# Pairing the short last tiles of two experts in one turn of a mixture-of-experts kernel

## The chip, the cores and the metric

The kernel runs on one core of a Trainium2 chip. The core has five engines that work side by side, each through its own queue in its own order: TensorE (PE in the profile; its weight loads have a row of their own, PEld), VectorE (DVE), ScalarE (ACT), GpSimd (POOL) and SyncE (SP). They hand work to each other through semaphores; 16 DMA engines move data between the device memory and the on-chip memory, on queues that SP, ACT and POOL feed. The metric is device time in microseconds (us), the median of several executions. One further execution is recorded by the hardware profiler, and all rows below come from that one.

## The reference

The input x has 2 sequences of 2048 tokens, 256 features each, in fp32: 4096 tokens. Three blocks follow each other, each on a layer-normed x and added back to x:

```python
x = x + 0.5 * ffn(layernorm(x))
x = x + attn(layernorm(x))
x = x + 0.5 * ffn(layernorm(x))
```

`ffn` is a mixture of 8 experts with top-1 routing. A token's expert is the argmax of 8 router logits; its own layer norm, a 256 to 1024 matrix W1 with bias and relu, a 1024 to 256 matrix W2 with bias, and the router's probability as a gate follow, all of that one expert:

```python
idx = argmax(softmax(xt @ Wr + br));  gates = max(softmax(...))
h = relu(xn @ W1[idx] + b1[idx])
y = (h @ W2[idx] + b2[idx]) * gates
```

`attn` is no attention but three layers of a gated linear recurrence over time (short convolution, two gates from 64x64 matrices, a scan, an output matrix, an RMS norm), between a 256 to 64 and a 64 to 256 projection. It needs the tokens in their order of time, while the ffn needs them sorted by expert.

How many tokens an expert gets is known only at run time. On the inputs drawn here the router sends 332, 17, 1583, 15, 1969, 2, 0 and 178 tokens to the eight experts in the first ffn, and 265, 27, 1637, 9, 1972, 1, 0 and 185 in the second.

## The kernel before

**Turns.** An expert's tokens are cut into tiles of P = 128. A tile is worked off in one turn of the generator `expert_tiles` (L1124), in three steps. `gathered` (`fetched`, L764, then `turned`, L820) gathers the tile's rows and its expert's weights W1 (with both biases, 1.18 MB) by indirect DMAs from POOL, normalises the rows on ACT (`z`, L825), transposes them on TensorE (`tpe`, L828) and scales them on DVE into `xT`. `hidden` (L845) multiplies them by W1 into PSUM (`ph`, L854) and applies bias and relu, by turns on ACT (L866) and DVE (L868), into `hT`. `finish` (L871) multiplies by W2, which for all eight experts stays in SBUF as `w2_sb` and is addressed through a register (`py`, L879), adds the bias (L887), gates and adds the residual (L888), and scatters the rows to their tokens by an indirect DMA (L890). TensorE works in the order hidden(j+1), transposes of j+2, finish(j). Buffers: four W1 tiles (`wp`), four row tiles (`xes`, XB), two of each `hT`, `xT` and `z`, three PSUM banks for `ph`, one for `py`.

**How many turns.** `NJ` = 39 bounds the number of tiles that 4096 tokens of 8 experts can need. The first ffn always runs `SURE` = 37 turns, the second 37; two tiles that the first may have over share the first two turns of the second, and two more turns of the second stand in branches that run only if the count calls for them. So 74 turns run.

**Which rows.** `First` (L390) works out for the whole input, before any turn, which tokens fill which tile: logits, one-hot experts, counts and ranks by matrix products (`Ranks`, L300), a number for each tile in the order in which tiles are opened (`count`), and from it the tables `idx` (token of each row), `sidx` (row of its statistics in `x_stat`) and `wrow` (rows of W1). `Route` (L569) does the same for the second ffn, one group of 512 tokens at a time; `ready` turns as many tiles into tables as are sure to be full.

**The order of the work.** The recurrence goes through 8 groups (`Chunk`), of 256 steps of both sequences each. Group g loads its tokens from `x1`, the DRAM buffer that the first ffn's turns scatter to, after as many turns as are sure to hold all of its tokens (`opened_by`: 11, 15, 19, ...), then `LAG` = 2 more turns are written down, then the group's projection (`down`, L1010, with `pd`, L1024) and its three layers. The framework takes this program order as priority and fixes each engine's order when the kernel is built. What is left of the turns is written down after the last group. So the run has a front (routing, no turns), a stretch of turns alone, a middle in which turns fill TensorE between the recurrence's steps, and a tail of turns alone. Waiting instructions hold up all that stands behind them on their engine; on POOL those are the gathers and scatters of other turns.

**Matmuls narrower than the array.** Two places write only some of the 128 output partitions: the router's logits in quarters of 32 (L229) and `pd` in halves of 64 (L1024).

Of the kernel before, what the change touches and what calls it, by code (L numbers as in the profile page):

```python
# [21 lines left out]
G = 4  # L22
# [28 lines left out]
def opened_by(n):  # L51

    return min(NJ, (n + E * (P - 1)) // P)
# [12 lines left out]
OWN = 3  # L66
EARLY = filled_by((NG - 1) * G * P)


SPARE = 2  # L70
SURE = NJ - SPARE
NS = NJ + SPARE


@with_exitstack
def macaron_kernel(
# [4 lines left out]
    w2: bass.AP,  # L81
# [88 lines left out]
    XB = 4  # L170
# [72 lines left out]
    class Choice:  # L243
# [48 lines left out]
        def sums(self):  # L292

            ex = self.tile([P, self.M, E], "ex")
            self.exp = nc.scalar.activation(ex, self.lo, AF.Exp)
            nc.vector.tensor_reduce(self.m[:, 1, :], ex, AX.X, ALU.add)
            nc.vector.reciprocal(self.m[:, 1, :], self.m[:, 1, :])
            return self.m[:, 1, :]

    class Ranks:  # L300
# [4 lines left out]
        def __init__(self, tile, M, oh, tiles, at, number, zero_one, all_ones, rk):  # L305
# [20 lines left out]
            place = cnt[:, 1]  # L326
            now = self.now = tiles[:, :, 1 : 1 + M]
            nc.vector.tensor_scalar(now, cnt[:, 0], SHIFT, None, ALU.arith_shift_right)
            opened = tile([P, M, E], "opened")
            nc.vector.tensor_tensor(opened.rearrange("p i e -> p e i"), now, tiles[:, :, 0:M], ALU.subtract)  # L330
            count = self.count = tile([P, M, E], "count")
# [10 lines left out]
            )  # L342

# [18 lines left out]
    def sort_into(got, lh, i0, n, tiles, first_one, last_one):  # L362


        hit, col, row = tiles
        nc.vector.tensor_tensor(
            hit,
            lh[:, 0, :, None].to_broadcast([P, n, NJ]),
            iota[:, None, 1 : 1 + NJ].to_broadcast([P, n, NJ]),
# [11 lines left out]
        for i in range(n):  # L381
            nc.tensor.matmul(
                got[:, 0 : 2 * NJ],
# [6 lines left out]
    class First:  # L390
# [5 lines left out]
        def __init__(self, pool):  # L396
            self.stores = []
            self.w2 = []
# [20 lines left out]
            xgs = [group_tile(), xpool.tile([P, G, D], F32, tag="u", name="u", bufs=1)]  # L419
            xgs += [Lane(0).tile([P, G, D], "x1"), group_tile(), Lane(1).tile([P, G, D], "x1")]  # L420
            for k in (2, 1):
                both = wp.tile([P, W1ROW], F32, tag="w1", name="x67")
                xgs += [
                    both[:, i * G * D : (i + 1) * G * D].rearrange("p (n d) -> p n d", d=D) for i in range(k)
                ]
# [26 lines left out]
            r = Ranks(tile, M, oh, tiles, at, number, flat(zero_one), all_ones, rk)  # L452


            pairs = tile([P, M, E], "pairs")
# [14 lines left out]
            by_turn = tile([P, H, NJ], "by_turn")  # L470
            turns = lane.bank([P, NJ], "turns")
            for a in range(H):
                nc.vector.tensor_scalar(
                    by_turn[:, a, :],
                    iota[:, 1 : 1 + NJ],
# [10 lines left out]
            wrow = kept([P, NJ], "wrow")  # L486
# [4 lines left out]
            got = bank("py", [P, 2 * NJ], "got")  # L491
            n = 2 * G
            for i in range(0, M, n):
                pieces = (
                    pool.tile([P, n, NJ], BF16, tag="f_hit", name="hit", bufs=2),
                    pool.tile([P, n, 2, NJ], BF16, tag="f_col", name="col", bufs=2),
# [5 lines left out]
            token = tile([P, NJ], "token")  # L502
            nc.vector.tensor_scalar(token, got[:, 0:NJ], float(P), float(FAR), ALU.mult, ALU.add)
            idx = kept([P, NJ], "idx")
            nc.vector.tensor_tensor(idx, token, got[:, NJ : 2 * NJ], ALU.add)
            at_p = tile([P, NJ], "at_p")
            nc.vector.tensor_scalar(at_p, got[:, NJ : 2 * NJ], float(NT), 2.0 * NT, ALU.mult, ALU.add)
            sidx = kept([P, NJ], "sidx")
            nc.vector.tensor_tensor(sidx, at_p, got[:, 0:NJ], ALU.add)
# [18 lines left out]
            with tc.issue_after(r.found.ins):  # L528
# [5 lines left out]
            self.idx = [(idx[:, j : j + 1], NG - 1) for j in range(NJ)]  # L534
            self.sidx = [sidx[:, j : j + 1] for j in range(NJ)]
            self.wrow = [wrow[:, j : j + 1] for j in range(NJ)]
            self.w2at = [(w2at, j, SURE) for j in range(SURE)]

            nc.vector.scalar_tensor_tensor(
                sidx[:, SURE:NJ], idx[:, SURE:NJ], -float(T), sidx[:, SURE:NJ], ALU.add, ALU.max  # L540
            )
            self.late_wrow, self.late_at = wrow[:, SURE:NJ], at[:, SURE:NJ]
# [3 lines left out]
    def second_weights(turns, kept, late=None):  # L546
# [4 lines left out]
        if late is not None:  # L551
            nc.vector.scalar_tensor_tensor(
                at[:, 0:SPARE], turns[:, 0:SPARE], float(W2ROW // P), late, ALU.mult, ALU.add
            )
# [14 lines left out]
    class Route:  # L569
# [5 lines left out]
        def __init__(self):  # L575
            self.stores = []
            self.idx, self.wrow, self.w2at, self.w2 = [], [], [], []
# [16 lines left out]
        def add(self, g, xg):  # L594
# [51 lines left out]
            if last:  # L646
                n += E
                nc.vector.tensor_tensor(filled[:, M, :], tiles[:, :, M], fills[:, :, M], ALU.subtract)
                nc.vector.tensor_copy(pairs[:, 1, M, :], new[:, :, M])
# [14 lines left out]
            )  # L664
            slots_of = pairs[:, 1, 0:M, :].rearrange("p i e -> p e i")
# [15 lines left out]
            by_turn = lane.tile([(1 + M) * E, 2, NS], "by_turn")  # L681
            for a, v in ((0, cst[0:n, C_EV : C_EV + 1]), (1, of_pair[0:n, 1:2])):
                nc.vector.tensor_scalar(
                    by_turn[0:n, a, :],
                    iota[0:n, 1 + SURE : 1 + SURE + NS],
# [5 lines left out]
            got = lane.bank([P, 2 * NJ + 2 * NS], "got")  # L691
# [13 lines left out]
            new_sum = cpool.tile([P, 2 * NJ + 2 * NS], F32, tag=f"sum{g % 2}", name="sum")  # L705
# [10 lines left out]
        def ready(self, upto, group):  # L716
# [3 lines left out]
            if n <= 0:  # L720
                return

            def kept(shape, name, dt=I32):
                return cpool.tile(shape, dt, tag=f"{name}1_{j0}", name=name)

            wrow = kept([P, n], "wrow")
# [4 lines left out]
                self.turns[0:1, 0, j0:upto], kept, first.late_at if j0 == 0 else None  # L731
            )
            if j0 == 0:
# [532 lines left out]
```

## Time and profile before

| | us |
|---|---|
| median of 3 runs | 772.67 (771.89 to 780.03) |
| the profiled execution's own time | 772.9 |
| its span, first to last instruction | 770.9 |
| busy: PE / PEld / DVE / ACT / POOL | 705.9 / 618.8 / 453.2 / 343.8 / 312.8 |
| mean granted TensorE clock | 0.966 |

A matmul of fp32 is two records in the profile: `ph` has 2368 records for 74 turns (32 each) and `py` 1184 (16 each). A record's duration holds its latency; how fast they follow each other is read from the timeline, where a row gives the start, the length and how many records it merges ("x32"). A busy time is the union of its records. "[0.30 <-issue]" at a row's end is idle time of the engine before it and what ended it.

### The profile page before, as it was taken

Reading aid. Unit: us, or ns where it says so; the run is one execution under the profiler, and the core shown is the slowest. Engines: PE = TensorE matmul, PEld = TensorE weight load, DVE = VectorE, ACT = ScalarE, POOL = GpSimd, SP = SyncE. Lnnn points to the kernel's source line nnn. Section 1 sums busy time; section 2 is a strip of 40 time slices with the busy share of each in tenths; the row PEclk is TensorE's granted clock in tenths of the full one; section 3 lists DMA queues with packets and bytes.
Section 4 is the critical chain, followed back from the end, with each engine's and each line's share of the span. In section 5 each row is a group of like instructions: output and inputs, shape, how many; then the busy total and the mean of one; then the engine's idle time right before and its main releaser. Section 6 shows DMA issues by size and latency. Waiting matters only on the chain. (4 is left out here: it accounts for less than half of the span.)

```text
span 770.9 us, 14129 instructions
## 1 busy us (share of the span) xinstructions
PE 705.9 (92%) x4785; PEld 618.8 (80%) x4785; DVE 453.2 (59%) x1674; ACT 343.8 (45%) x772; POOL 312.8 (41%) x319
## 2 busy tenths in 40 slices
PE   9639999979999989999998898898999899999995
PEld 6438999968778878878886796787878898999994
DVE  7653434345588677686885866767668433344341
ACT  4323323226566753757656576455552222223220
POOL 4444555524434334353365333133432433434432
PEclk9859999989999999999999999899999999999998
DMA  9986555544526334263344534343533556455430
GB/s 332 408 219 206 171 201 210 181 153 145 177 80 207 148 131 148 77 225 122 131 164 158 171 116 138 104 151 109 211 129 135 194 190 218 163 219 193 164 127 8
DMA packets 36808, 129.75 MB, mean 168 GB/s; under 512 B 7282, under 2 KB 21888, under 8 KB 26240
## 3 DMA queue, kind: packets, MB, share of 16 engines
q0 software_dynamic: 19584, 104.51, 39.3%
q1 hardware_dynamic: 16720, 23.93, 9.1%
q8 instruction: 42, 0.69, 0.4%
q10 hardware_dynamic: 432, 0.37, 0.2%
q14 instruction: 30, 0.25, 0.1%
HBM read 118.19 MB, written 16.38 MB: 175 GB/s over the span
## 5 line engine op out<-in xcount | busy, mean ns | idle before, releaser
L854 PE MATMUL ph<-xT,w 128*128 128x128 f32 x2368 | 303.2, 281 | 2.1 <-ACT hT L866 1.0
L854 PEld LDWEIGHTS ph<-xT,w 128*128 128x128 f32 x2368 | 290.4, 195 | 13.4 <-issue 5.6
L879 PE MATMUL py<-w_sb,hT 128*128 x1184 | 280.5, 382 | 1.1 <-DVE ye L887 0.6
L879 PEld LDWEIGHTS py<-w_sb,hT 128*128 128x128 f32 x1184 | 215.8, 190 | 29.8 <-issue 4.4
L794 POOL DMA_INDIRECT w<-w_rows_dram,wrow x76 | 78.7, 1035 | 329.0 <-issue 142.1
L866 ACT ACTIVATE hT<-ph,w 128x128 f32<-128x128 f32 x296 | 106.7, 366 | 136.3 <-PE ph L854 69.3
L868 DVE TENSOR_SCALAR hT<-ph,w 128x128 f32<-128x128 f32 x296 | 102.0, 347 | 110.2 <-ACT hT L866 99.1
L825 ACT ACTIVATE z<-xe 128x256 f32<-128x256 f32 x74 | 44.3, 599 | 172.4 <-DMA xe<-xa,idx 88.0
L887 DVE TENSOR_TENSOR ye<-py,w 128x256 f32<-128x256 f32 x74 | 31.1, 421 | 77.3 <-PE py L879 66.9
L832 DVE TENSOR_SCALAR xT<-tpe,par 128x128 f32<-128x128 f32 x148 | 57.2, 404 | 25.5 <-PE tpe L828 25.2
L774 POOL DMA_INDIRECT xe<-x_in_dram,idx x39 | 42.3, 1084 | 24.7 <-issue 8.3
L890 POOL DMA_INDIRECT x<-ye,idx x39 | 40.7, 1045 | 20.2 <-issue 6.5
L890 POOL DMA_INDIRECT out_dram<-ye,idx x37 | 37.9, 1024 | 24.6 <-DVE ye L888 15.1
L774 POOL DMA_INDIRECT xe<-x_stat,sidx x39 | 39.6, 1017 | 14.2 <-issue 11.3
L774 POOL DMA_INDIRECT xe<-xa,idx x39 | 40.6, 1040 | 11.9 <-issue 10.7
L828 PE MATMUL tpe<-cst,z 128*128 128x128 f32 x148 | 29.3, 279 | 9.7 <-ACT z L825 9.7
L888 DVE SCALAR_TENSOR_TENSOR ye<-ye,xe 128x256 f32<-128x256 f32 x74 | 35.6, 481 | 1.6
L1047 DVE SCALAR_TENSOR_TENSOR xc<-xb,par,xc 128x256 f32<-128x256 f32 x72 | 34.5, 480 | 0.5
L1054 ACT ACT_TABLE_LOAD x21 | 26.9, 1283 | 13.3 <-PE pm L1052 11.5
L215 ACT COPY uT<-tp 128x512 f32<-128x512 f32 x40 | 22.4, 586 | 21.4 <-PE tp L213 21.1
L1067 ACT ACT_TABLE_LOAD x22 | 28.2, 1283 | 0.4
L828 PEld LDWEIGHTS tpe<-cst,z 128*128 128x128 f32 x148 | 18.8, 144 | 10.9 <-ACT z L825 10.7
(211 smaller groups left out, 740.2 us busy)
## 6 DMA issues: line engine op xcount, KB each, us to landing
w_sb<-w_dram SPq DMA_DIRECT2D x8, 1024.0 KB, 16.0
xa<-xg SPq DMA_DIRECT2D x16, 259.0 KB, 5.0
x<-x SPq DMA_DIRECT2D x16, 256.0 KB, 3.1
x<-x_in_dram SPq DMA_DIRECT2D x10, 256.0 KB, 5.5
xa<-cst SPq DMA_DIRECT2D x2, 1036.0 KB, 17.7
w<-w_rows_dram,wrow POOLq DMA_INDIRECT x76, 6.1
xg<-x_in_dram SPq DMA_DIRECT2D x4, 256.0 KB, 4.8
xe<-x_in_dram,idx POOLq DMA_INDIRECT x39, 4.1
```

The costliest lines, as they stand in the source:

```text
L774: got = nc.gpsimd.indirect_dma_start(out=xe[:, a:b], out_offset=None, in_=src, in_offset=bass.IndirectOffsetOnAxis(ap=at, axis=0), bounds_ ...
L794: nc.gpsimd.indirect_dma_start(out=w1[:], out_offset=None, in_=w1_rows, in_offset=bass.IndirectOffsetOnAxis(ap=r.wrow[j], axis=0), bounds_ ...
L825: nc.scalar.activation(z, xe[:, 0:D], AF.Identity, scale=scale, bias=shift)
L828: nc.tensor.transpose(tp[:, c, :], z[:, c * P : (c + 1) * P], ident)
L832: nc.vector.tensor_scalar(xT[:, c, :], tp[:, c, :], par[:, P_G + c : P_G + c + 1], par[:, P_B + c : P_B + c + 1], ALU.mult, ALU.add,)
L854: nc.tensor.matmul(ph[:, q, :], lhsT=w1[:, c * F + f * P : c * F + (f + 1) * P], rhs=xT[:, c, :], start=(c == 0), stop=(c == C - 1),)
L866: nc.scalar.activation(hT[:, f, :], ph[:, q, :], AF.Relu, bias=b1)
L868: nc.vector.tensor_scalar(hT[:, f, :], ph[:, q, :], b1, 0.0, ALU.add, ALU.max)
L879: nc.tensor.matmul(py, lhsT=hT[:, f, :], rhs=w2_sb[:, bass.ds(r.w2[j] + f * D, D)], start=(f == 0), stop=(f == FC - 1),)
L888: nc.vector.scalar_tensor_tensor(ye, ye, gate, xe[:, 0:D], ALU.mult, ALU.add)
L890: made = nc.gpsimd.indirect_dma_start(out=dst, out_offset=bass.IndirectOffsetOnAxis(ap=at, axis=0), in_=ye, in_offset=None, bounds_check=T ...
L1047: nc.vector.scalar_tensor_tensor(xc, self.xb[:, k : k + GT], cw(k), xc, ALU.mult, ALU.add)
```

## The change

Tiles that are the last of their expert and hold fewer than 64 tokens are *short*. Up to six short tiles per ffn are taken out of the ordinary numbering and put by twos into three *mixed* turns. In a mixed turn, rows 0 to 63 belong to one expert and rows 64 to 127 to another. Each matmul writes 64 output partitions, half of TensorE's columns: in `hidden` one per half of the hidden units and per expert, so 64 products with 64 stationary and 64 moving columns in place of 16 of 128 by 128; in `finish` 16 of 64 rows by 256 in place of 8. The first expert's W2 comes from `w2_sb`, the second's by a third gather, `w2b`, into a buffer of `wp`; a mixed turn so gathers 1.18 + 1.18 + 1.05 MB, and gathers and scatters its rows in halves, with an indirect DMA each.

With the mixed turns, `NF` = 35 bounds the ordinary tiles. The first ffn runs 31 ordinary and 3 mixed turns, the second 31 and 3; the rest stands in branches. On the inputs above either ffn has 37 tiles, six of them short: 31 and 3 hold them all. Mixed turns are the 5th, 8th and 11th turn of the first ffn, as their tokens may belong to any group, and stand among the last ten of the second. Group g is loaded after 14, 18, 22, ... turns.

Other parts: a turn's rows are issued a turn ahead of its weights (`rows`, `weights`, `then_weights`); XB is 5; the bias of W2 and the residual are combined before `py` is there, by a DVE operation at the end of `hidden` (it is then the W1 buffer's last reader), and one DVE operation is left after `py`; `LAG` is 1; `OWN`, the group from which tables of the second ffn are made, is 2 in place of 3; the front's scratch tiles share buffers in another way.

```diff
-OWN = 3
-SPARE = 2
-SURE = NJ - SPARE
-NS = NJ + SPARE
+OWN = 2
+HALF = P // 2
+MIXED = 3
+U = 2 * MIXED
+NF = (T + max(E * (HALF - 1), (E - U) * (P - 1))) // P
+NC = NF + U
+SPARE = 4
+SURE = NF - SPARE
+NS = NF + SPARE
+NSC = NS + U
+LAST = 31
...
-    XB = 4
+    XB, YB = 5, 5
...
+    def short_tiles(tile, held, now, start):
+        used = tile([P, E], "used")
+        nc.vector.scalar_tensor_tensor(used, now, -float(P), held, ALU.mult, ALU.add)
+        is_short = tile([P, E], "is_short")
+        nc.vector.tensor_scalar(is_short, used, float(HALF), None, ALU.is_lt)
+        nth = tile([P, E], "nth_short")
+        nc.vector.tensor_tensor_scan(nth, ones[:, 0:E], is_short, 0.0, ALU.mult, ALU.add)
+        paired, number = tile([P, E], "paired"), tile([P, E], "pair_at")
+        nc.vector.scalar_tensor_tensor(paired, nth, U + 0.5, is_short, ALU.is_lt, ALU.mult)
+        nc.vector.scalar_tensor_tensor(number, nth, float(start), paired, ALU.add, ALU.mult)
+        return paired, number
...
+            if short_from is not None:
+                paired, pair_at = short_tiles(tile, self.held, now[:, :, M - 1], short_from)
+                newest = tile([P, E], "newest")
+                nc.vector.tensor_tensor(newest, paired, now[:, :, M - 1], ALU.mult)
+                short = tile([P, M, E], "short")
+                nc.vector.tensor_tensor(short.rearrange("p i e -> p e i"), now,
+                    newest[:, :, None].to_broadcast([P, E, M]), ALU.is_equal)
+                nc.vector.tensor_tensor(short, short, opened, ALU.mult)
+                nc.vector.tensor_tensor(opened, opened, short, ALU.subtract)
...
+            if short_from is not None:
+                nc.vector.tensor_tensor(short, short, pair_at[:, None, :].to_broadcast([P, M, E]), ALU.mult)
+                numbers = at[:, :, 1 : 1 + M].rearrange("p e i -> p i e")
+                nc.vector.tensor_tensor(numbers, numbers, short, ALU.add)
...
+    def weights(r, j):
+        w1s, w2s = [], []
+        for t, h in tiles_of(j):
+            w1 = wp.tile([P, W1ROW], F32, tag="w1", name="w1")
             nc.gpsimd.indirect_dma_start(
                 out=w1[:],
...
+            w1s.append(w1)
+            if h == 1:
+                w2b = wp.tile([P, W1ROW], F32, tag="w1", name="w2b")
+                nc.gpsimd.indirect_dma_start(
+                    out=w2b[:, 0:W2ROW],
...
     def hidden(tile_in):
...
+                if len(w1s) == 1:
+                    steps = [[(w1s[0], slice(0, P), slice(0, P))]]
+                else:
+                    lo, hi = slice(0, HALF), slice(HALF, P)
+                    steps = [[(w1s[0], lo, lo), (w1s[1], hi, hi)], [(w1s[0], hi, lo), (w1s[1], lo, hi)]]
+                for step in steps:
+                    for c in range(C):
+                        for w1, rows_of, of in step:
+                            at = c * F + f * P
+                            nc.tensor.matmul(
+                                ph[rows_of, q, of],
+                                lhsT=w1[:, at + rows_of.start : at + rows_of.stop],
+                                rhs=xT[:, c, of],
...
+        ye = hp.tile([P, D], F32, tag="ye", name="ye", bufs=YB)
+        for h, w1 in enumerate(w1s):
+            of = slice(h * n, (h + 1) * n)
+            with tc.issue_after(made.ins):
+                nc.vector.scalar_tensor_tensor(
+                    ye[of, :], w1[of, C * F + FC :], gate[of, :], xe[of, 0:D], ALU.mult, ALU.add
+                )
+        return hT, ye
...
     def finish(r, j, tile_in, made):
...
+            for k, (t, h) in enumerate(tiles_of(j)):
+                of = slice(k * n, (k + 1) * n)
+                at = slice(f * D, (f + 1) * D)
+                nc.tensor.matmul(
+                    py[of, :],
+                    lhsT=hT[:, f, of],
+                    rhs=w2s[k][:, at] if h == 1 else w2_sb[:, bass.ds(r.w2[t] + f * D, D)],
...
-        nc.vector.tensor_tensor(ye, py, w1[:, C * F + FC :], ALU.add)
-        nc.vector.scalar_tensor_tensor(ye, ye, gate, xe[:, 0:D], ALU.mult, ALU.add)
+        with tc.high_priority(AHEAD):
+            nc.vector.scalar_tensor_tensor(ye, py, gate, ye, ALU.mult, ALU.add)
...
+        def then_weights(j):
+            late = j + 1 < n and turns[j + 1][0].by_fill and turns[j + 1][1] in second.begins
+            upto = min(j if late else j + 1, n - 1)
+            while len(xe_got) <= upto:
+                ahead.append(rows(*turns[len(xe_got)]))
+            with tc.issue_after(xe_got[-1].ins):
+                return weights(*turns[j])
...
-    LAG = 2
+    LAG = 1
...
+    turns = [(first, j) for j in range(SURE)]
+    for m, pair in enumerate(pairs_of(NF)):
+        turns.insert(4 + 3 * m, (first, pair))
+    turns += [(second, j) for j in range(LAST)]
+    at = len(turns) - 3 * MIXED + 2
+    for m, pair in enumerate(pairs_of(NS)):
+        turns.insert(at + 3 * m, (second, pair))
...
-        advance(opened_by((g + 1) * G * P) - done)
+        advance(opened_by((g + 1) * G * P) + MIXED - done)
```

293 lines of the change are left out of this document (165 added, 128 removed).

## The prediction

> **What bounds the kernel now.** I read the slices first, then the groups, then the timeline of the tail. The slices say where TensorE is full, the groups how little it waits, the timeline what a turn costs.
>
> ```profile
> PE   9639999979999989999998898898999899999995
> L854 PE MATMUL ph<-xT,w 128*128 128x128 f32 x2368 | 303.2, 281 | 2.1 <-ACT hT L866 1.0
> L879 PE MATMUL py<-w_sb,hT 128*128 x1184 | 280.5, 382 | 1.1 <-DVE ye L887 0.6
> ```
>
> ```profile
> 685.21 3.73 PE L854 MATMUL ph<-xT,w 128*128 128x128 f32 x32
> 688.78 0.38 PE L828 MATMUL tpe<-cst,z 128*128 128x128 f32 x2
> 689.00 3.62 PE L879 MATMUL py<-w_sb,hT 128*128 x16
> 692.46 3.73 PE L854 MATMUL ph<-xT,w 128*128 128x128 f32 x32
> ```
>
> TensorE is the bound in both stretches of turns alone (62 to 153 us, and from 603 on). There a turn takes 692.46 - 685.21 = 7.25 us: 3.57 for hidden, 0.22 for the transposes, 3.46 for finish. A hidden record takes 107 ns, a finish record 216. In the middle the recurrence's own chain adds waits.
>
> **Turns that go.** 74 turns become 62 ordinary and 6 mixed ones. Were a mixed turn as long as an ordinary one, six turns would go. By the fixed order of TensorE's instructions in the two programs, the first group's first transposes stand after 13 finishes before and after 15 now; the last group's `second.add` after 49 and 51. The middle so keeps its turns, the first stretch gains 2, the tail loses 8. Both are stretches at 7.25: 6 x 7.25 = **-43.5**.
>
> **What a mixed turn costs more.** Do halves of the array run side by side? Two places of this kernel use parts of it:
>
> ```profile
> 212.35 1.09 PE L1024 MATMUL pd<-uT,down_sb 128*64 128x256 f32 x8 [0.70 <-ACT uT L215]
> ...
> 237.24 0.31 PE L382 MATMUL got<-col,row 128*128 128x78 bf16 x4
> ...
> 370.86 0.42 PE L229 MATMUL pl<-uT,wr_c 128*32 128x128 f32 x8
> 371.22 0.49 PE L854 MATMUL ph<-xT,w 128*128 128x128 f32 x2
> ```
>
> One `pd` record lasts 0.38 (its median), so seven starts take 1.09 - 0.38 = 0.71: 101 ns each, where a full-width record of as many columns takes 216. Halves do overlap. Quarters too: (0.42 - 0.27) / 7 = 21 ns for 107. Finish of a mixed turn is 32 such records in 16 pairs of 216: 3.46, nothing more. Hidden is 128 records of 64 columns each: 53 ns of streaming, by twos, 3.4 us. But TensorE must also be fed: four records of L382 take (0.31 - 0.20) / 3 = 37 ns each, and 128 x 37 = 4.7. No row shows a long run of short half records, so the bounds are 3.4 and, if each took the 107 ns of an ordinary one, 13.7. I take 4.2, by the two nearest rows: +0.6. Changing between full and partial width costs too: eight quarters need 0.21 but the next full record starts 0.36 after their first (371.22), about 0.1 is lost ahead of them and 0.1 on the next record: 0.35 for in and out, twice per mixed turn, 0.7. So 1.3 x 6 = **+8** (3 to 11 without the first rival below).
>
> The Trainium skill has a rule against this. "TensorE: Matmul & The Clock Gate", section "Wait — 56ns, not 53.3ns?", gives a sequencer cost of about 62 ns per matmul instruction when hardware decoding is off, which binds where array work is shorter. By it, 128 records would be an estimated 7.9 us, and the sum 22 us higher. L382's 37 ns speaks against it here, in a run of four only.
>
> **The front.** `short_tiles` and what follows it add six DVE operations on 128x8 and five on 128x256. Rows for these: L469 0.16, L354 0.41; 6 x 0.16 + 5 x 0.41 = 3.0 on the chain to `idx`. Before, turn 0's `z` waited for the rows of `x_stat`, issued only at 51.16, as the statistics' store had to land; the tokens' rows went out at 47.58. In the changed program the statistics are finished right after `new`, about 2 us earlier. Then rows go out at 47.6 + 3.0 + 1.3 = 51.9 for the statistics, 0.7 later than before, behind rows that land at 54.7 instead of 51.7. `z` goes from 53.5 to about 55: **+1.5** (0 to 3).
>
> **POOL in the first stretch.**
>
> ```profile
> 71.34 0.99 POOL L794 DMA_INDIRECT w<-w_rows_dram,wrow  x1 [7.49 <-issue]
> 72.64 1.03 POOL L890 DMA_INDIRECT x<-ye,idx  x1 [0.30 <-issue]
> 73.97 1.05 POOL L774 DMA_INDIRECT xe<-x_in_dram,idx  x1 [0.30 <-issue]
> 75.33 0.99 POOL L774 DMA_INDIRECT xe<-x_stat,sidx  x1 [0.31 <-issue]
> 78.60 0.99 POOL L794 DMA_INDIRECT w<-w_rows_dram,wrow  x1 [2.28 <-issue]
> ```
>
> Each issue takes 1.3, an ordinary turn four. A mixed turn of the first ffn has nine: 4 of rows, 3 of weights, 2 scatters. Of three turns with one mixed, POOL needs 17 x 1.3 = 22.1, TensorE 2 x 7.25 + 8.55 = 23.05. No row shows an issue of 64 rows (0 to 1.3); I take 1.3. POOL keeps up, barely: **+2** of small waits (0 to 5).
>
> The first mixed turn (number 4, from 0) is worse. In POOL's new order the token rows of turns 5 and 6 stand ahead of its weights, as does a scatter. Turn 6's rows go into turn 1's buffer (five buffers), which is free after turn 1's last DVE operation: its finish ended at 77.4, plus 0.5, plus the front's 1.5: 79.4. Then rows, scatter, statistics, each 1.3: W1 gathers at 83.3 and 84.6. One lands 6.1 after issue (median), so 90.7, and up to 2.9 later as they share the DMA engines (1.18 MB at the 408 GB/s of the fullest slice). TensorE, at 84.4 before, wants them at 85.9. Wait: **+6** (0 to 8), and the clock: after idle stretches it drops (mean 0.56 from 50 to 62 us, 0.95 from 153 to 216), **+2** (0 to 3.4). The later pairs have three turns of lead; I find no wait there. The mixed turns of the tail need 2 + 3 + 2 issues, three turns 13 x 1.3 = 16.9, which fits, and the two more doubled turns at the start of the second ffn fall into the middle, where POOL was busy for 36.6 of 110 us. Behind the waiting gather on POOL stand scatters and the rows of the next turns, which have slack of a turn by then.
>
> **The groups' loads.** A group's load waits for the scatters of its turns. It now has one turn less as cover, LAG being 1.
>
> ```profile
> 154.45 3.71 PE L879 MATMUL py<-w_sb,hT 128*128 x16
> 158.63 0.44 PE L213 MATMUL tp<-cst,x 128*128 128x128 f32 x2 [0.47 <-DMA x<-x]
> 159.31 0.87 PE L213 MATMUL tp<-cst,x 128*128 128x128 f32 x6 [0.24 <-DMA x<-x]
> ```
>
> Group 0's transposes already wait 0.7, so a turn less is up to 7.25 of wait; the scatter leaves about 0.5 earlier as it no longer stands behind a held W1 gather, and this load took 6.3, against a median of 3.1; SP fills five groups of `xa` beside it now, four before. **+5** (0 to 8). Groups 1 to 3 had 5.1, 4.9 and 6.7 between landing (198.9, 242.1, 285.0) and first transpose (204.0, 247.0, 291.7); a turn of the middle is some 10 us, and their scatters left 2.8 to 5.7 after their finish where I count 1.8. **+4** together (0 to 12). From group 4 on the new order leaves two turns.
>
> **Gains beside it.** Rows ahead of weights end waits for `z`: TensorE waited 9.7 for it, 5.3 of that at turn 0; **-3** (-4.4 to 0). One DVE operation less at the end: **-0.4**. The W1 buffer's earlier release is worth nothing to TensorE in the tail, where gathers land 7 us ahead of need. What a mixed turn adds on DVE and ACT lies beside its 8.55 on TensorE: eight half evictions of about 0.3 on each in place of four of 0.35, one more DVE operation of 0.48; with the 0.06 by which the new operation after `py` (0.48) is longer than the old (0.42), 1.5 per mixed turn would be the price if that cover were gone.
>
> **Sum.** 770.9 - 43.5 + 8 + 1.5 + 2 + 6 + 2 + 5 + 4 - 3 - 0.4 = 752.5 of span. The profiled execution took 772.9, 2.0 more than its span, and the median is 772.7: about **754**.
>
> **Rivals.** *Half records don't keep their pace (slower than before).* Place: hidden of the six mixed turns. If each of the 128 records takes 107 ns, hidden is 13.7, 9.5 over my 4.2: 754 + 57 = 811. It makes the kernel slower by 1% from (780.4 - 754) / 6 = 4.4 more per mixed turn, that is 67 ns a record. For: no row shows a long run of them, and weight loads of 64 columns (0.136) are not half of those of 128 (0.19). Against: the overlaps above.
>
> *The feeding eats it.* Hidden at 4.7 (+3), all POOL, load and clock terms at their upper bounds (+5, +3 and +1.4, +11) and the front at 3.0 (+1.5), no gain from rows (+3): 754 + 28 = 782 at worst, some 770 for half of it. For: POOL at 22.1 of 23.05. Against: the bounds are not all met at once.
>
> *It does not do what it says*, as tiles are not short: the counts exclude it, both ffns have six short tiles and 31 others, so no branch runs.
>
> *All hidden.* The waits fall where TensorE waits for the recurrence anyhow: 754 - 19 = 735.
>
> **How the numbers follow.** A measurement of this kernel tells about 1% from no change: 764.9 to 780.4 is the same. Forecast with its terms a little up or down (740 to 765) 0.62; all hidden 0.12; feeding (765 to 780) 0.15, beyond that 0.03; half records 0.08. Faster 0.74, same 0.15, slower 0.11. The range leaves out half of the hidden case and the far end: 738 to 772.
>
> **What would show it.** Right: 16 pairs of `py` records in about 3.5 us in a mixed turn, hidden of 3.5 to 4.7; turns of 7.25 between them; a wait of TensorE for a W1 DMA at turn 4, near 86 us; a wait for `x1` at the first group; the tail's last ten turns without waits. Wrong: hidden of a mixed turn above 6 us, waits for weights at every mixed turn, or a middle that takes more than 440 us from the first group's transposes to the last `second.add`.

## The result and the profile after

The changed kernel takes 817.78 us (median of 4, 809.03 to 823.66), the kernel before 772.28 beside it: ratio 1.048, 95% interval 1.036 to 1.061. Two of the four, the profiled one among them, came out more than 1.5% above the fastest and are left out of the ratio, so the medians alone would give more. It is slower by 4.8%, where the prediction had 754. The profiled execution took 823.7, span 821.9, mean granted clock 0.923.

From the page of the changed kernel, the slices and the two groups that answer to those shown of before:

```profile
PE   9455896989899999889969888989898995998994
PEld 6345785869688787778757777868777875877783
...
PEclk9757987989899999999999999998899898998998
...
L938 PE MATMUL ph<-xT,w 128*128 128x128 f32 (+1 forms) x2752 | 305.2, 276 | 36.5 <-issue 19.3
...
L983 PE MATMUL py<-w_sb,hT 128*128 (+1 forms) x1088 | 271.3, 395 | 8.3 <-issue 5.7
```

Hidden (L938) has twelve turns of full records less, with six mixed turns in their place, and is no less busy (305.2 us for 303.2); it now has 36.5 us of idle time before it, where it had 2.1. 19.3 of that is "issue": TensorE waited for nothing that the profile shows. From the timeline of TensorE, the first mixed turn of the tail:

```profile
712.68 3.62 PE L983 MATMUL py<-w_sb,hT 128*128 x16
716.23 1.90 PE L938 MATMUL ph<-xT,w 128*64 128x64 f32 x50
718.53 0.41 PE L938 MATMUL ph<-xT,w 128*64 128x64 f32 x6 [0.40 <-issue]
719.30 0.43 PE L938 MATMUL ph<-xT,w 128*64 128x64 f32 x6 [0.36 <-issue]
720.06 0.44 PE L938 MATMUL ph<-xT,w 128*64 128x64 f32 x6 [0.32 <-issue]
720.82 0.40 PE L938 MATMUL ph<-xT,w 128*64 128x64 f32 x5 [0.32 <-issue]
721.56 0.22 PE L938 MATMUL ph<-xT,w 128*64 128x64 f32 x1 [0.34 <-issue]
722.26 3.24 PE L938 MATMUL ph<-xT,w 128*64 128x64 f32 x54 [0.49 <-issue]
725.44 0.53 PE L904 MATMUL tpe<-cst,z 128*128 128x128 f32 x2
```

Fifty half records come at full pace: less the last one's latency of 0.22, 49 starts in 1.68 us, 34 ns each. Then six come every 0.76 us, with gaps between; each record is a matmul with a weight load of its own, so that is 12 instructions in 0.76 us, 63 ns each. That is the quickest that such a stretch gets; in others 1 to 5 records stand between gaps as long or longer. Then 54 come without a gap. All six mixed turns have such gaps, and four of them end in 52 to 60 records without one. From first to last start their hidden takes 11.95, 12.29, 10.72, 8.97, 9.26 and 6.45, in all 59.6 us, where I had 4.2 each.

Finish of a mixed turn is as forecast, two records at a time, 216 ns from pair to pair after the first (32 records, 733.14 to 736.43):

```profile
733.14 0.43 PE L983 MATMUL py<-w_sb,hT 128*64 x1
733.15 0.43 PE L983 MATMUL py<-w2b,hT 128*64 128x256 f32 x1
733.41 0.38 PE L983 MATMUL py<-w_sb,hT 128*64 x1
733.41 0.38 PE L983 MATMUL py<-w2b,hT 128*64 128x256 f32 x1
```

### The profile page after: what moved, and what is told of

It reads as the page before. It is cut to its first block, busy times and chain, and to the rows that moved or that the text cites. A ratio compares the mean times of both kernels' runs of the same rounds, so it can differ in the third digit from the quotient of the medians.

```text
span 821.9 us, 14834 instructions
## 1 busy us (share of the span) xinstructions
PE 701.9 (85%) x5157; PEld 594.8 (72%) x5157; DVE 447.0 (54%) x1682; ACT 329.9 (40%) x762; POOL 318.2 (39%) x332
## 4 chain that ended last, share of the span: by engine, by line
PE 54%; issue 13%; DVE 13%; DMA 7%; ACT 5%; POOL 4%; another core or an unknown queue 2%; SPq 0%; ACTq 0%; POOLq 0%; DVEq 0%
PE ph L938 24%; PE py L983 17%; DMA x<-x 3%; PE tpe L904 2%; PE tp L223 2%; PE po L1179 2%; DMA w<-w_rows_dram,wrow 2%; PE pm L1156 2%; PE pd L1128 1%; POOL rs L657 1%; ACT L1171 1%; DVE hT L955 1%; DVE h L1175 1%; POOL xe L842 1%
## 5 line engine op out<-in xcount | busy, mean ns | idle before, releaser
L938 PE MATMUL ph<-xT,w 128*128 128x128 f32 (+1 forms) x2752 | 305.2, 276 | 36.5 <-issue 19.3
L938 PEld LDWEIGHTS ph<-xT,w 128*128 128x128 f32 (+1 forms) x2752 | 284.2, 188 | 60.0 <-issue 49.2
L983 PE MATMUL py<-w_sb,hT 128*128 (+1 forms) x1088 | 271.3, 395 | 8.3 <-issue 5.7
L983 PEld LDWEIGHTS py<-w_sb,hT 128*128 128x128 f32 (+1 forms) x1088 | 200.6, 193 | 41.2 <-issue 12.5
L953 ACT ACTIVATE hT<-ph,w 128x128 f32<-128x128 f32 (+1 forms) x296 | 102.4, 356 | 269.4 <-PE ph L938 94.6
L955 DVE TENSOR_SCALAR hT<-ph,w 128x128 f32<-128x128 f32 (+1 forms) x296 | 96.7, 335 | 136.3 <-ACT hT L953 112.0
L991 DVE SCALAR_TENSOR_TENSOR ye<-py,xe,ye 128x256 f32<-128x256 f32 x68 | 32.6, 480 | 43.3 <-PE py L983 39.9
L963 DVE SCALAR_TENSOR_TENSOR ye<-w,xe 128x256 f32<-128x256 f32 (+1 forms) x74 | 35.0, 473 | 0.2
L1179 PE MATMUL po<-h,rec_sb 128*128 128x256 f32 x48 | 17.7, 452 | 16.7 <-DVE h L1175 16.0
L657 POOL TENSOR_TENSOR rs<-ve,power 128x8 f32<-128x8 f32 x8 | 14.6, 1822 | 39.4 <-DVE ve L271 39.3
```

What stands on the lines that cost most here:

```text
L938: nc.tensor.matmul(ph[rows_of, q, of], lhsT=w1[:, at + rows_of.start : at + rows_of.stop], rhs=xT[:, c, of], start=(c == 0), stop=(c == C ...
L953: nc.scalar.activation(hT[:, f, of], ph[:, q, of], AF.Relu, bias=b1)
L955: made = nc.vector.tensor_scalar(hT[:, f, of], ph[:, q, of], b1, 0.0, ALU.add, ALU.max)
L963: nc.vector.scalar_tensor_tensor(ye[of, :], w1[of, C * F + FC :], gate[of, :], xe[of, 0:D], ALU.mult, ALU.add)
L983: nc.tensor.matmul(py[of, :], lhsT=hT[:, f, of], rhs=w2s[k][:, at] if h == 1 else w2_sb[:, bass.ds(r.w2[t] + f * D, D)], start=(f == 0), s ...
L1179: nc.tensor.matmul(po, lhsT=rec_sb[:, l, 2, :], rhs=h, start=True, stop=True)
```

## The experiments

The gaps turned out to depend on the chip, so the runs are told with their chips, A to D. The four kernels on A ran beside each other, as did the three on C and the three on D; B was met four times: with after_again and w1_first_lag2, with after_third and w1_first_again, with the two before_ kernels, and with lag2_again and lag2_wide. One program differs between two of these occasions on B by 9 to 11 us (the changed kernel 819.54 and 808.75; w1_first_lag2 and lag2_again, which are the same program, 804.02 and 795.19). "Mixed hidden" sums the six mixed turns, first to last start, with their waits for W1 and their stretches at half clock; "issue" is TensorE's wait of that name ahead of hidden.

| chip | run | median us | ratio to before (95%) | mixed hidden | issue |
|---|---|---|---|---|---|
| A | w1_first | 759.99 | 0.980 (0.972 to 0.988) | 25.9 | none |
| A | no_pairs | 766.75 | 0.995 (0.991 to 0.999) | | none |
| A | wide_hidden | 778.47 | 1.009 (1.005 to 1.013) | 49.3 | none |
| A | double_stream | 777.72 | 1.007 (1.003 to 1.011) | 45.6 | none |
| B | after_again | 819.54 | 1.057 (1.050 to 1.064) | 58.7 | 19.2 |
| B | after_third | 808.75 | 1.044 (1.036 to 1.052) | 58.5 | 19.9 |
| B | w1_first_again | 812.49 | 1.050 (1.043 to 1.056) | 60.0 | 19.8 |
| B | w1_first_lag2 | 804.02 | 1.040 (1.033 to 1.047) | 59.3 | 18.6 |
| B | lag2_again | 795.19 | 1.029 (1.023 to 1.035) | 56.4 | 18.0 |
| B | lag2_wide | 797.69 | 1.028 (1.018 to 1.037) | 51.0 | 1.7 |
| B | before_halves_2 | 847.05 | 1.098 (1.077 to 1.119) | | 8.1 |
| B | before_same_2 | 776.94, one run | | | 0.6 |
| C | double_stream_2 | 815.40 | 1.052 (1.038 to 1.066) | 64.7 | 10.5 |
| C | wide_hidden_2 | 799.08 | 1.031 (1.024 to 1.039) | 47.9 | none |
| C | no_pairs_2 | 779.16 | 1.007 (1.000 to 1.014) | | none |
| D | after_fourth | 763.12 | 0.990 (0.983 to 0.997) | 27.0 | none |
| D | before_halves | 801.72 | 1.040 (1.036 to 1.044) | | 0.5 |
| D | before_same | 769.40, one run | | | 0.8 |

The kernel before took 771 on A, 771 to 773 on B, 774 on C and 771 on D.

### What the parts cost: four kernels on chip A

*wide_hidden*: the mixed hidden in full width, half the instructions.

```diff
-                    steps = [[(w1s[0], lo, lo), (w1s[1], hi, hi)], [(w1s[0], hi, lo), (w1s[1], lo, hi)]]
+                    steps = [[(w1s[0], both, lo)], [(w1s[1], both, hi)]]
```

> A mixed turn's hidden is made of 32 matmuls with all 128 columns of W1 and 64 moving columns, in place of 64 with 64: half the instructions, nothing side by side. Theory 1 (TensorE can't be handed that many short instructions: 256 weight loads and matmuls per mixed hidden): 128 instructions are at most what had queued up when the gaps began (some 100 to 190), so hidden becomes 64 records x 107 ns = 6.9 us with few or no gaps, 41 in all six in place of 59.6, and the half-clock spells behind the gaps go: 790 to 805 us. Theory 2 (half records are slow in the array itself, 75 ns each on average): hidden also becomes 6.9, without gaps. The run prices the pairing with a plain hidden; a time still above 810 would say that hidden is not where the time goes.

*double_stream*: twice the columns per half matmul, the same number of instructions.

```diff
-                                ph[rows_of, q, of],
+                                ph[rows_of, q, :],
...
-                                rhs=xT[:, c, of],
+                                rhs=xT[:, c, :],
```

> Each half matmul of a mixed turn's hidden moves all 128 columns in place of 64 (of each product only half is of use, and the second pair of products overwrites columns of the first, so the mixed rows come out as other numbers). Twice the streaming, the same 256 instructions. Theory 1 (supply of instructions): the streaming is 128 x 107 / 2 = 6.9 us, still under what hidden takes now, so hidden stays at 6.9 to 12 and the whole within 1% of the changed kernel, 810 to 825 us. Theory 2 (each half record is slow by what it streams or by the sharing of the array): hidden doubles, to some 13 to 24 us, and the whole is 845 to 880.

*no_pairs*: the rest of the change without mixed turns.

```diff
-MIXED = 3
+MIXED = 0
...
-SPARE = 4
+SPARE = 2
...
-LAST = 31
+LAST = 37
```

> The changed kernel with MIXED = 0, SPARE = 2, LAST = 37: no tile shares a turn, 74 ordinary turns as before; rows ahead of weights, LAG 1, OWN 2, five row buffers and the early DVE operation stay. Theory 1 (front 9 us late and the middle 24 us longer come from these other parts): 772 + 9 + 24 = 805, at least 795. Theory 2 (the mixed turns bring all of it): 770 to 780.

*w1_first*: turn 1's weights ahead of the rows of turns 1 and 2.

```diff
-        ahead = [rows(*turns[0]), rows(*turns[1])]
+        ahead = [rows(*turns[0])]
+        w1_of_1 = weights(*turns[1])
+        ahead.append(rows(*turns[1]))
...
-        w1 = then_weights(1)
+        w1 = w1_of_1
```

> The changed kernel with turn 1's weights issued on POOL before the rows of turns 1 and 2. Theory 1 (TensorE's two waits at turn 1, 8.8 and 4.9 us, are W1 standing behind four row gathers on POOL): turn 2's finish comes at 82 to 85 in place of 91.7 and the whole is 7 to 9 us shorter, 800 to 812. Theory 2 (the wait is for the statistics and the tokens' rows, or turn 4 loses it again, since its weights are then what TensorE waits for): within 3 us of the changed kernel.

All four came out below every range given, and w1_first 2.0% below the kernel before. The reason is in w1_first's timeline: the mixed turn whose hidden took 8.97 us in the result has no gap here, and 128 half records in 3.73 us, 29 ns each.

```profile
666.52 3.95 PE L938 MATMUL ph<-xT,w 128*64 128x64 f32 x128
670.40 0.44 PE L904 MATMUL tpe<-cst,z 128*128 128x128 f32 x2
```

Either the edit of the first turns had done that, or the chip. wide_hidden and double_stream, with 7 to 8 us in most of their mixed turns, take 18 us more than w1_first; their mixed hidden is 23 and 20 longer (in wide_hidden 6 of it in one turn, with a wait for W1 and the clock at half).

### The program or the chip

The changed kernel unedited, and w1_first with LAG = 2:

> The changed kernel itself, unedited, once more on a chip on which other kernels of this study ran. In the kernel with turn 1's weights first, the same 128 half records of a mixed hidden took 3.7 to 5.2 us, with no gaps after the first two, where the changed kernel's took 6.5 to 12.3. Theory 1 (the gaps belong to that execution's chip or run: TensorE was short of instructions there and is not here): hidden of mixed turns at 3.7 to 5.5 here, and the whole at 760 + 8 for the front, 762 to 775. Theory 2 (the gaps belong to this program, to where its instructions lie): the gaps are there again and the whole is 805 to 825.

> Turn 1's weights first, as before, and LAG = 2 again: one turn more between a group's load and its first use. Theory 1 (LAG 1 costs waits for x1 at the first groups, as predicted 5 + 4, TensorE's waits for x being 6.1 us in all in that kernel): those waits go, 3 to 9 us less, 750 to 757. Theory 2 (the turn written down later only shifts the middle, and the recurrence's chain sets it): within 3 us of 760, or up to 7 above.

Both had gaps in all six mixed turns. w1_first was then run beside the changed kernel:

> The kernel with turn 1's weights first, once more, beside the changed kernel on one chip: its mixed turns ran without gaps on one chip, the changed kernel's and the LAG = 2 variant's with gaps on another. Theory 1 (the gaps go by the program): 753 to 763 us here, no gaps. Theory 2 (they go by the chip): as the changed kernel beside it, both with gaps (800 to 815) or both without (755 to 765).

> The changed kernel, unedited, beside the one with turn 1's weights first on one chip. Theory 1 (the gaps go by the program): gaps in every mixed turn, 810 to 824 us. Theory 2 (they go by the chip): the same picture as beside it, without gaps 762 to 775 us.

The same w1_first that took 760 on A takes 812 on B, with 60.0 us of mixed hidden in place of 25.9. So the gaps go by the chip, not by the program (that a chip keeps its kind is shown on B alone, on four occasions; A, C and D were met once each), and the edit of w1_first shows no gain: on A its finish of turn 2 starts at 82.8, which met the expectation, but the unedited kernel's does so at 82.7 on D, and w1_first's at 92.1 on B. Turn by turn, w1_first on B is later than on A by 9.3 at turn 1, 20.8 more by the last mixed turn of the first ffn, 5.3 in the middle and 13.8 in the tail's mixed turns; in the stretches of turns alone the other turns agree within 0.7.

### Instructions or streaming, on a chip with gaps

Chip C has them too, though the changed kernel itself did not run there:

> Half records of 128 moving columns in the mixed hidden (256 instructions, 6.9 us of streaming), a second time, as the first time fell on a chip on which the mixed turns have no gaps. If this chip has the gaps: theory 1 (instructions come too slowly, about 62 ns each in the stretches with gaps) gives the same 256 instructions and so hidden of 6.9 to 12 us as with 64 columns, still with gaps, and 800 to 825 us in all; theory 2 (a limit on the array's work, a throttle) gives twice the time of the 64-column records, 13 to 24 us, and 845 or more. On a chip without gaps: 772 to 783 as the first time.

> The mixed hidden of 32 full-width matmuls (128 instructions, 6.9 us of streaming), a second time. If this chip has the gaps: theory 1 (supply of instructions) gives about half the time spent in gaps or none, hidden 6.9 to 8, and 780 to 800 us; theory 2 (a throttle of the array) gives gaps as in the half records, hidden 9 to 13, and 805 to 825. On a chip without gaps: 775 to 785.

> No mixed turns, 74 ordinary ones, a second time. An ordinary turn has about 114 instructions of TensorE in 7.25 us, 64 ns each. If this chip has the gaps: theory 1 (supply of instructions) gives 762 to 785, since ordinary turns just fit; theory 2 (this chip is slower in everything that the change reorders, the front above all) gives 785 to 800. On a chip without gaps: 762 to 773.

The first mixed turn of the tail in double_stream_2, then in wide_hidden_2:

```profile
703.73 4.92 PE L938 MATMUL ph<-xT,w 128*64 128x128 f32 x72
709.54 3.29 PE L938 MATMUL ph<-xT,w 128*64 128x128 f32 x56 [0.89 <-issue]
```

```profile
695.58 7.25 PE L938 MATMUL ph<-xT,w 128*128 128x64 f32 x64
702.67 0.39 PE L904 MATMUL tpe<-cst,z 128*128 128x128 f32 x2
```

Twice the streaming with the same 256 instructions leaves the sum at 64.7, against 58.5 to 60.0 with single streaming on B, with half as much "issue" (10.5 for 19 to 20) and no gap in the last mixed turn; half the instructions leave no gap. That is nearer to theory 1, by which the number of instructions sets the time: theory 2 had 13 to 24 per turn and 845 or more, and only two turns, 13.3 and 14.2, are above 12. Number and width are not told apart here, since the runs with many short records are those with half records; that width alone does not do it is seen in the finish of the mixed turns, half records without a gap. But wide_hidden_2 was at the upper end of its range and 21 above wide_hidden without any gap in hidden, and no_pairs_2 is 12 above no_pairs: chips with gaps take more than the gaps. The next kernels asked for more instructions without mixed turns, on the kernel before:

```diff
                 for c in range(C):
-                    nc.tensor.matmul(
-                        ph[:, q, :],
-                        lhsT=w1[:, c * F + f * P : c * F + (f + 1) * P],
...
+                    for h in (0, 64):
+                        nc.tensor.matmul(
+                            ph[h : h + 64, q, :],
+                            lhsT=w1[:, c * F + f * P + h : c * F + f * P + h + 64],
```

> The kernel before, with one edit: each matmul of hidden is made of two, of 64 stationary columns and all 128 moving ones, side by side in the two halves of TensorE's columns. No pairing of experts, no other order, the same results; 64 weight loads and matmuls more per turn (about 114 become 178), no more streaming. Theory 1 (on a chip with gaps TensorE gets an instruction only every 45 to 62 ns once its queue is used up): 178 x 45 to 62 = 8.0 to 11.0 us per turn of the tail in place of 7.25, and 820 to 1000 us in all; on a chip without gaps 7.3 to 7.9 us per turn and 772 to 810. Theory 2 (the gaps come with something else of the mixed turns: two experts' weights, three gathers, half evictions): no gaps on either chip, 772 to 810.

> The kernel before, unedited, profiled beside the others. Its turn 1 took no longer than 8.5 us of TensorE in the profile shown. Theory 1 (the 8 us that turn 1 of the changed kernel stands still on a chip with gaps come from the chip and the changed order together): no such wait here on either kind of chip, 770 to 776. Theory 2 (a chip with gaps has that wait in any kernel): a wait of 5 to 9 us between the hidden of turn 0 and that of turn 1, made up later.

> The changed kernel, unedited, beside the other two. On a chip with gaps 805 to 824 us as three times before; on one without 755 to 770 (the kernel with turn 1's weights first took 760 on one), hidden of the mixed turns then 3.7 to 5.3 us.

> The kernel before with hidden in column halves, a second time; the first fell on a chip without gaps (7.47 us per turn of the tail, 802 us). If this chip has the gaps: theory 1 (the number of TensorE's instructions alone brings them) gives 8.0 to 11.0 us per turn of the tail and 830 to 1000 us; theory 2 (the gaps need the mixed turns) 7.5 per turn and 800 to 808. On a chip without gaps: 800 to 804.

> The kernel before, unedited, profiled beside it. If this chip has the gaps: theory 1 (the stall at turn 1 comes from the chip and the changed order together) gives hidden of turn 1 within 2 us of the end of turn 0's, 770 to 777; theory 2 (any kernel has it on such a chip) a wait of 5 to 9 us there.

D has no gaps. There the changed kernel takes 763.12, 1.0% below the kernel before (interval 0.3 to 1.7). before_halves takes 801.7 on D and 847.1 on B: the same program, 45 us apart, without any mixed turn. So more and narrower matmuls in hidden are enough to bring a cost on such a chip. The size that I expected is refuted, though: in the tail on B most turns take 7.47 as on D (178 instructions, 42 ns each) and every fourth some 0.3 more, and the 47 us come about before: 13 by the start of finish 15 (counted from 0), 34 from there to finish 49. So there is no steady limit of 62 ns. That a store of instructions runs out, which a burst of 256 in 3.7 us empties, fits the gaps, but is argued, and waits named "issue" are only 10 of the 47 us. This is TensorE in before_halves_2, by what it waited for:

```profile
PE po L1076 <- DVE h L1072: 12.3, 12, 3.5
PE ph L855 <- issue: 8.1, 18, 1.0
```

TensorE's signals come late there, too. Here are, in the same run, the wait of ACT that is released by a signal with no instruction just ended ("remote"), then the transposes of a turn and the DVE operation that they release:

```profile
ACT hT L867 <- remote: 112.6, 41, 4.1
93.77 0.44 PE L828 MATMUL tpe<-cst,z 128*128 128x128 f32 x2
97.50 0.41 DVE L832 TENSOR_SCALAR xT<-tpe,par 128x128 f32<-128x128 f32 x1 [3.73 <-remote]
```

The transposes end at 94.21 and `xT` starts 3.3 later; in before_halves on D it starts 0.04 after (89.69 and 89.73). Every run on B and C, and the result, has such waits of ACT and DVE for `hT` and `xT` (from 7.7 us in before_same_2 to 178 here); no run on A or D, nor the profile of before ahead of the change, has one. A store that runs empty ahead of TensorE gives no reason for a late signal behind it; something that fills up behind TensorE could be a reason for both. No run separates the two, and that the late signals make up the 34 us in the middle is argued.

The stall at turn 1 is not the change's. before_same_2 on B has it as well, 5.3 us from the end of turn 0's hidden to the first record of turn 1's, and so theory 2 of its expectation holds; in order, hidden of turn 0, the transposes of turn 1, and what then waits, the `xT` that these transposes release among it:

```profile
55.05 5.18 PE L854 MATMUL ph<-xT,w 128*128 128x128 f32 x32 [0.50 <-DVE xT L832]
60.07 0.38 PE L828 MATMUL tpe<-cst,z 128*128 128x128 f32 x2
61.33 1.14 PE L879 MATMUL py<-w_sb,hT 128*128 x4 [0.88 <-ACT hT L866]
64.99 0.41 DVE L832 TENSOR_SCALAR xT<-tpe,par 128x128 f32<-128x128 f32 x1 [2.48 <-remote]
65.50 0.76 PE L854 MATMUL ph<-xT,w 128*128 128x128 f32 x2 [3.03 <-ACT hT L866]
```

The transposes end at 60.45 and `xT` starts at 64.99, a late signal again; on D they end at 62.12, `xT` starts at 62.67 and the same two records of hidden at 63.18. The changed order makes it longer (8.80 in the result, 5.91 in no_pairs_2, both as a wait for `xT`).

### LAG, and a way out

> Turn 1's weights first and LAG = 2, a second time; on a chip with gaps it took 804 us, 8 less than the same with LAG = 1 there. Theory 1 (LAG 1 is a part of the change that costs, whatever the chip): on a chip without gaps 8 less than the 760 of LAG = 1, so 749 to 756, below both kernels; on one with gaps 800 to 808. Theory 2 (the 8 us were the chip's): 757 to 765 without gaps.

> The same with the mixed hidden of 32 full-width matmuls: half the instructions, 7.0 us in place of 3.7 without gaps or about 10 with them. Theory 1: on a chip without gaps 6 x 3.2 = 19 more than its neighbour in this call, 768 to 776; on one with gaps 12 to 18 less than its neighbour, 785 to 793, still above the kernel before.

Both fell on B. LAG = 2 ended the waits for x1 at the groups, 4.1 us, and took those for the recurrence's `h` from 16.0 to 5.8, while those for W1 rose from 6.4 to 13.5 (w1_first_again against w1_first_lag2). The spans are 808.5 and 799.6, 8.9 less, but this pair did not run beside each other, and a program differs by as much between two occasions on B; beside the changed kernel, w1_first_lag2 took 15.5 less. So LAG 1 costs something on this chip, and how much is open. On a chip without gaps LAG 2 was not run. lag2_wide refutes its expectation of 12 to 18 less: the waits "issue" fall from 18.0 to 1.7, but the full-width hidden needs 7.0 without gaps, and the tail's half records needed 6.4 to 7.8 with them. No kernel tried is below the kernel before on a chip with gaps; on those without, w1_first (2.0%), the changed kernel (1.0%) and no_pairs (0.5%) are.

## Why the prediction was wrong

The two kinds of chip separate two errors. By the starts of finishes on one chip (before_same against after_fourth, D; bounds are finish 2, then 13 and 15, then 49 and 51, then the last) and, beside it, what a chip with gaps adds (after_third on B against after_fourth):

| stretch | predicted | D | more on B |
|---|---|---|---|
| front, to finish of turn 2 | +1.5 | +2.0 | +8.4 |
| to the first group's work | +33.5 | +25.4 | +17.4 |
| middle | +1 | +11.5 | +4.7 |
| tail | -54.4 | -45.3 | +13.2 |
| after the last finish | 0 | +2.3 | -0.2 |
| span | -18.4 | -4.1 | +43.5 |

(33.5 = two turns 14.5 + mixed turns 4 + POOL 2 + turn 4 and clock 8 + group 0 5; +1 = groups 4 less rows 3; -54.4 = -58 for eight turns, +4 for mixed turns, -0.4 for the last operation.)

Of the 43.5 that B takes more, 31.5 are mixed hidden (58.5 for 27.0) and 8.4 the front with its stall at turn 1. On D 763.12 lies in my range of 738 to 772, but partly by luck: the first stretch came out 8 shorter than I had, middle and tail 10.5 and 9 longer.

**The step that failed** is "Hidden is 128 records of 64 columns each": 4.2 us by four records of L382 at 37 ns. On D they take 3.73 to 4.11 (7.61 in the first, a wait for W1 included) and the step holds; there a mixed turn and the one behind it take 686.89 - 671.79 = 15.10, 0.6 over two ordinary ones, where I had 1.3. In the result they average 59.6 / 762 = 78 ns a record, past the 67 from which my first rival decided: 34 us more than my 4.2 each. Four records can't show it: on such a chip 35 to 95 records come fast before the first gap. I gave that rival 0.08 because the row was short but fast; the right reading was that the row tells nothing on the 128. That the rival's 811 is near the result is luck: it had 107 ns a record, and the other 30 us of the miss come from elsewhere, the front, the middle and the tables below.

The Trainium skill, "TensorE: Matmul & The Clock Gate", "Wait — 56ns, not 53.3ns?", gave about 62 ns per matmul with hardware decoding off, which I set aside. In the result's first tail turn the stretch with gaps has 63 ns per instruction, but with weight loads counted, so 126 per matmul; and on A and D, and in the tail of before_halves_2 on B, the same instructions come faster. No run here shows which way of decoding is on, so that the rule is at work here is not shown.

**Turn 4's wait for W1** was there on D as worked out, but shorter, 2.02 us; in the result turn 1's stall had already given the gathers their time (W1 issued at 85.26, first record at 95.21):

```profile
86.22 0.33 PE L938 MATMUL ph<-xT,w 128*64 128x64 f32 x2
88.56 5.49 PE L938 MATMUL ph<-xT,w 128*64 128x64 f32 x126 [2.02 <-DMA w<-w_rows_dram,wrow]
```

**The first group's load** costs less than I said: its transposes wait 3.67 for x on D, where before_same waits 1.42, so 2.3 more in place of 5 (in the result 3.99).

**The tail's eight turns** are gone, but 12 us of them came back, by something that I did not look at: by `filled_by` the second ffn has tables for 21 tiles before the last group's are made, and its 22nd tile is now turn 55 (counted from 0), where it was turn 58. TensorE runs out of turns that it may start. Here is its timeline on D at that point, the last tables being made at 640.4, and then, from the view of the line that makes the tables (L810), who waited for them in all. In no_pairs, on A, nothing did.

```profile
640.58 3.26 PE L983 MATMUL py<-w_sb,hT 128*128 x14 [1.78 <-DVE idx L810]
645.53 0.44 PE L904 MATMUL tpe<-cst,z 128*128 128x128 f32 x2 [1.69 <-ACT z L901]
645.81 0.60 PE L983 MATMUL py<-w_sb,hT 128*128 x2
651.67 5.49 PE L938 MATMUL ph<-xT,w 128*128 128x128 f32 x32 [5.26 <-DMA w<-w_rows_dram,wrow]
```

```profile
who waited for it (us, times):
  POOL xe L842: 18.0, 4
  POOL out_dram L994: 8.4, 1
  PE py L983: 1.8, 1
```

From finish 53 to 57 the four turns take 676.0 - 635.2 = 40.8 in place of 29.0. Part of the middle's +11.5 lies where the second ffn begins, three turns earlier than before: finish 33 to 34 takes 22.3 on D and waits 4.25 for W1. That the tables are the cause there too is argued from the wait of POOL, not shown by an edit. LAG 1 alone does not make the middle longer on a chip without gaps: no_pairs has it too, and its 36 turns of the middle (finish 12 to 48) take 401.3 on A, where before_same takes 406.7 on D (13 to 49) and the changed kernel 418.3.

Of the other terms: with rows ahead the waits for `z` did fall (9.7 us before, 3.3 in no_pairs on A, all of it at turn 0), but what it is worth in time (-3) can't be told, no_pairs being 4 us below before on A and 5 above on C. POOL's 22.1 of 23.05 did not quite keep up: on D TensorE waits 2.47 and 1.74 for W1 in the turns behind the second and the third mixed turn (122.88 and 148.95), where I had found no wait, 4.2 for the +2. The clock I had lower after waits only; in the result it falls to half during or soon after five of the six mixed turns (0.923 in all).

## What to carry to other kernels

A short run of fast records does not show the pace of a long one (35 to 95 records at full pace here, then gaps): price many short matmuls by a long run, and count weight loads and matmuls beside the us. When turns are taken away from a pipeline that waits for data made elsewhere, look up which later turn first needs that data and how many turns stood between. When a result contradicts its own near relatives, run the same program on another chip before looking for the cause in the program.

## What was new about the hardware

Chips differ, most where TensorE's instructions are many: one and the same program takes 760 and 812 us on two of them, while the kernel before takes 771 to 774 on all four. On A and D 128 half records take 3.73 us, on B up to 12, and those of twice the columns 6.9 to 8.0 on A and up to 14 on C; the chip of the result is of the second kind by its gaps. TensorE's signals reach ACT and DVE late on B, on C and in the result, by 3 us and more at times, in kernels of ordinary turns too, and not on A and D. What is short there is open. The trace has TensorE's instructions arriving in packets of 16 KB (queue 8 of the DMA part, 45 packets, 0.74 MB), and in four of the six mixed turns of the result the gaps end 0.9 to 1.5 us before the next such packet starts (104.01 and 105.42, 722.26 and 723.76, 750.71 and 751.91, 778.49 and 779.43); in the other two the packet came before the gaps. The skill's "Runtime: NRT & Kernel Launch", "Instruction fetch mechanics", has these blocks of 16 KiB, fetched ahead and mostly hidden; on A and D, where there are no gaps, that agrees. On B and C the packets themselves take no longer: their median is 0.96 to 1.11 us there and 0.96 to 1.07 on A and D. So a slow transfer is not the cause; no run here tells a late request for it from a slow decoder or from something that fills up behind TensorE. Nor does any tell whether recording is what holds TensorE up there: each execution here has a granted clock beside its time, so none is known to have run unrecorded.

Two halves of the array with 128 moving columns each cost 0.22 us per turn against full width (7.47 for 7.25 in the tail of before_halves on D), the change of width included.
